# Prologue of an AdaLN and FFN kernel: agg_w in two halves around the second pair's layer 0, and W_up's load moved behind the second X

## The chip, the cores and the metric

The kernel runs on one core of one Trainium2 chip. The metric is the device time of one execution in microseconds. All data are float32. The engines are named as in the profile: PE is TensorE (PEld its weight loads), DVE is VectorE, ACT is ScalarE, POOL is GpSimd, and SP is SyncE, which only issues DMAs.

## The reference, cut to what matters

The input x has 128 samples of 64 channels and 1024 positions. Two residual layers follow each other.

```python
# layer 0: a channel mix of each sample's own, then a rank-128 product along the positions
att = softmax(mlp(cond_128))                         # 128 x 8
agg_w = einsum('bk,koi->boi', att, L0_cond_weight)   # one 64 x 64 matrix a sample
agg_b = att @ L0_cond_bias_k
y = einsum('boi,bih->boh', agg_w, x) + agg_b[:, :, None]
x = x + (y @ B) @ A.T + ffn_bias
# layer 1: a grouped convolution over 9 positions with a context a sample, then the FFN
c = conv1d(x, weight, groups=4, pad=4) + (cond_128 @ c_weight.T)[:, :, None] + fside[None, :, None]
top1 = argmax(c @ gate_w.T + expert_bias)
x = x + c @ W_up.T + lora(c, expert=top1)
```

W_up is 1024 x 1024. The kernel multiplies by its four quarters w11, w12, w21 and w22 and by sums of them (T1, T2, T3, -T4), with seven half-size products where eight would be plain.

## The kernel before, in words

Two samples make a pair of 128 rows, so there are 64 pairs, and two pairs make a group d of the FFN. Every engine's instructions stand in the order in which the program writes them: nothing is rescheduled, and each engine waits where its next instruction waits.

Layer 0 of a pair has three parts. `layer0_in` (L299) multiplies the transposed x (xt) by B in eight matmuls into pxb; ACT copies the result to xb. `layer0_mix` (L308) multiplies xb by the pair's block-diagonal agg_w into pz, and ACT or DVE makes z0 of it. `layer0_out` (L324) multiplies z0 by AT in two halves (pd), DVE adds each half to x, and SP stores it to a scratch tensor in HBM, x1d. Then SP loads it back in another layout, as X, in two DMAs (L339, L340), each of which waits for the store. The convolution `conv` works on X: pairs 0 and 1 take the plain form (L400), the later ones a form with differences made on POOL (`differences`, L355) and a shared part (`shared_in`, L366). There are three X buffers.

agg_w for all samples is made once, in `agg_all` (L273): att transposed (attT) times the weights wa in two halves of four matmuls, copied from PSUM by DVE and ACT into staging tiles and stored to HBM (`agg_out`), from where each group's matrices are loaded later (`load_cond`, L177). The first four pairs (FIRST) don't wait for this. `own_att` (L235) picks their att rows with one matmul, and `own_bd` (L248) sums their matrices in eight DVE instructions (L253 once, L255 seven times). `own_bias` (L242) makes their bias operand on ACT. `b_sums` (L225) makes the two sums of B that the biases need.

[...] Four rotate through `bank()` (pool ps); four are the FFN's accumulators, with the tags pb0 to pb3 (pool psb), which `ffn_a` (L445) first takes.

The prologue (L584 to L644) orders the loads. SP's queue carries the packed small weights, B, the first pair's xt and x, and AT; then the x1d and X transfers, smalld (the per-sample biases and contexts), their broadcasts bc, and w11. ACT's queue carries ffn_bias, xt1, wa, x1, ws, xt2 and x2. POOL's queue, after the two ffn_bias additions of pairs 1 and 2 (`add_fbias`, L550), carries w12, w22, w21, xt3, x3, gl (gate and LoRA A) and lb (LoRA B), in all 4.5 MB. The quarters' sums are made on DVE (`w_sum`, L142), and w12 lies in the buffers that the differences take later.

After the prologue a loop over d runs the FFN of group d beside layer 0 and the convolutions of the pairs to come.

Of the kernel before, what the change touches and what calls it, by code (L numbers as in the profile page):

```python
# [35 lines left out]
F32 = mybir.dt.float32  # L36
# [5 lines left out]
P = 128  # L42
# [4 lines left out]
NC = L // P  # L47
# [10 lines left out]
N = 512  # L58
GT = 64
NX = 3  # L60
NBD = 3
FIRST = 4
# [6 lines left out]
def block(ctx: ExitStack, tc: tile.TileContext, a: dict, out: bass.AP):  # L69
    nc = tc.nc  # L70
# [4 lines left out]
    psb = ctx.enter_context(tc.tile_pool(name="psb", bufs=1, space=PSUM))  # L75
# [15 lines left out]
    def bank(name):  # L91
        return ps.tile([P, 512], F32, tag="bank", name=name)

    def loaded(name, shape, src=None, tag=None, eng=nc.sync):
        t = const.tile(shape, F32, tag=tag or name, name=name)
        eng.dma_start(t, a[name] if src is None else src)
        return t
# [7 lines left out]
    def load_x(pr, eng=nc.gpsimd):  # L105
        xts[pr] = xtp.tile([P, NC, P], F32, tag="xt", name=f"xt{pr}")
        xs[pr] = xpool.tile([P, L], F32, tag="x", name=f"x{pr}")
        eng.dma_start(xts[pr], a["xt"][pr])  # L108
        eng.dma_start(xs[pr], a["x"][pr])
# [23 lines left out]
    def load_w(name, eng):  # L133
        W[name] = const.tile([P, HC, N], F32, name=f"w{name}")
        eng.dma_start(W[name], a[f"w{name}"])

    def load_w12(eng):
        for h in range(2):
            W12.append(tmp.tile([P, HC // 2, N], F32, tag=f"tmp{h}", name=f"w12_{h}"))
            eng.dma_start(W12[h], a["w12"][:, h * HC // 2 : (h + 1) * HC // 2])  # L140
# [20 lines left out]
    ones = const.tile([P, P], F32, name="ones")  # L161
# [12 lines left out]
    aggd = dram.tile([NB, CH, CH], F32, name="aggd")  # L174
    smalld = dram.tile([NB, 2, CH], F32, name="smalld")

    def load_cond(g):  # L177

        if g * GP >= FIRST:
            bds[g] = BD[g % NBD]  # L180
            for b in range(2):
                nc.sync.dma_start(
                    bds[g].rearrange("(r two) t b o -> two r t b o", two=2)[b, :, :, b, :],
                    aggd.rearrange("(t two) r o -> two r t o", two=2)[b, :, g * GP : (g + 1) * GP],
                )
        bcs[g] = bcp.tile([P, GP, 2, 2, CH], F32, tag="bc", name=f"bc{g}")
        nc.sync.dma_start(
            bcs[g].rearrange("p t b k o -> p (t b k o)"),
            smalld[2 * g * GP : 2 * (g + 1) * GP]
            .rearrange("b k o -> (b k o)")  # L190
            .unsqueeze(0)
            .partition_broadcast(P),
        )
# [29 lines left out]
    bred = const.tile([P, P], F32, name="bred")  # L223

    def b_sums():  # L225

        p = bank("pbsum")
        nc.tensor.matmul(p[:8, :P], ones[:, :8], bred, start=True, stop=True)
        nc.tensor.matmul(p[:, P : P + 1], bred, ones[:, :1], start=True, stop=True)
        nc.scalar.copy(bs8, p[:8, :P])  # L230
        nc.scalar.copy(bsum, p[:, P : P + 1])

    attx, bdx, mv = {}, {}, {}

    def own_att(pr):  # L235

        p = bank(f"pattx{pr}")
        nc.tensor.matmul(p[:, :8], sel[:, pr].rearrange("p o b -> p (o b)"), att[:, 0, :8], start=True, stop=True)
        attx[pr] = const.tile([P, 8], F32, name=f"attx{pr}")
        nc.vector.tensor_copy(attx[pr], p[:, :8])  # L240

    def own_bias(pr):  # L242

        mv[pr] = const.tile([8, 2, CH], F32, name=f"mv{pr}")
        for b in range(2):
            nc.scalar.activation(mv[pr][:, b], bk, AF.Copy, scale=attT[:8, 2 * pr + b : 2 * pr + b + 1])

    def own_bd(pr):  # L248
        bdx[pr] = const.tile([P, 2, CH], F32, name=f"bdx{pr}")
        for k in range(8):  # L250
            w = attx[pr][:, k : k + 1]
            if k == 0:
                nc.vector.tensor_scalar(bdx[pr], wk[:, k], w, None, ALU.mult)  # L253
            else:
                nc.vector.scalar_tensor_tensor(bdx[pr], wk[:, k], w, bdx[pr], ALU.mult, ALU.add)  # L255
# [5 lines left out]
    def condition_rest():  # L261

        p = bank("psmall")
        nc.tensor.matmul(p[:, :CH], attT[:8, :], bk, start=True, stop=True)
        nc.tensor.matmul(p[:, CH : 2 * CH], condT, cwT, start=True, stop=True)
        small = const.tile([NB, 2, CH], F32, name="small")
        nc.scalar.copy(small[:, 0], p[:, :CH])
        nc.vector.tensor_tensor(small[:, 1], p[:, CH : 2 * CH], fs, ALU.add)
        return small
# [3 lines left out]
    def agg_all():  # L273

        first = ytp.tile([NB, 4, 512], F32, tag="yt", name="agg0")
        second = [xpool.tile([NB, 2, 512], F32, tag="x", name=f"agg1{j}") for j in range(2)]
        for h in range(2):
            ps4 = [bank(f"pagg{h}_{j}") for j in range(4)]
            for j in range(4):
                rows = slice(32 * j, 32 * (j + 1))  # L280
                nc.tensor.matmul(ps4[j], attT[rows, :], wa[rows, h], start=True, stop=True)
            for j in range(4):
                to = second[j // 2][:, j % 2] if h else first[:, j]
                if j % 2:
                    nc.scalar.copy(to, ps4[j])
                else:
                    nc.vector.tensor_copy(to, ps4[j])
        to = aggd.rearrange("b i o -> b (i o)").rearrange("b (j h n) -> h b j n", j=4, h=2)
        aggs.extend([(to[0], first), (to[1][:, :2], second[0]), (to[1][:, 2:], second[1])])

    def agg_out():
        for to, agg in aggs:
# [12 lines left out]
        nc.scalar.copy(xb, pxb[:, :P])  # L305
        xbs[pr] = xb

    def layer0_mix(pr):  # L308
        g, t = pr // GP, pr % GP
        own = pr < FIRST  # L310
        pz = bank(f"pz{pr}")
        bd = bdx[pr] if own else bds[g][:, t]
        nc.tensor.matmul(pz[:, :P], xbs.pop(pr), bd.rearrange("p b o -> p (b o)"), start=True, stop=not own)  # L313
        z0 = z0p.tile([P, P], F32, tag="z0", name=f"z0_{pr}")
        to = z0.rearrange("k (o b) -> k b o", b=2)
        pzv = pz[:, :P].rearrange("k (b o) -> k b o", b=2)
        if own:
            nc.tensor.matmul(pz[:, :P], bs8, mv[pr].rearrange("k b o -> k (b o)"), start=False, stop=True)
            nc.scalar.copy(to, pzv)  # L319
        else:  # L320
            nc.vector.scalar_tensor_tensor(to, bcs[g][:, t, :, 0, :], bsum, pzv, ALU.mult, ALU.add)
        z0s[pr] = z0

    def layer0_out(pr):  # L324
        x, z0 = xs[pr], z0s.pop(pr)
        xt = X[pr % NX]
        d = x1d.tile([Q, P, P], F32, tag="x1d", name=f"x1d{pr}")
        dv = d.rearrange("q (c g) m -> (q c) g m", g=BG)
        h = P // 2
        for hf in range(2):  # L330
            cols = slice(hf * 512, (hf + 1) * 512)
            qs = slice(hf * Q // 2, (hf + 1) * Q // 2)
            pd = bank(f"pd{pr}_{hf}")
            nc.tensor.matmul(pd, z0, at[:, cols], start=True, stop=True)  # L334
            nc.vector.tensor_tensor(x[:, cols], pd, x[:, cols], ALU.add)  # L335
            nc.sync.dma_start(
                d[qs].rearrange("q r m -> r q m"), x[:, cols].rearrange("r (q m) -> r q m", m=P)
            )
        nc.sync.dma_start(xt[h:, :, :P], dv[:h])  # L339
        nc.sync.dma_start(xt[:h, :, 1 : P + 1], dv[h:])  # L340
# [87 lines left out]
    def conv(pr):  # L428
        for b in range(2):
            conv_in(pr, b)  # L430
            conv_out(pr, b)
# [117 lines left out]
    def add_fbias(pr, eng):  # L549
        eng.tensor_tensor(xs[pr], xs[pr], fbias, ALU.add)  # L550

    def layer0(pr):
        layer0_in(pr)
        layer0_mix(pr)
        layer0_out(pr)
# [38 lines left out]
    turn_att()  # L594
    own_bias(0)
    layer0_in(0)
    b_sums()
    own_bd(0)
    add_fbias(0, nc.vector)
    layer0_mix(0)  # L600
    small = condition_rest()
    load_x(2, nc.scalar)
    layer0_out(0)
    nc.sync.dma_start(smalld, small)
    load_cond(0)
    load_w("11", nc.sync)

    add_fbias(1, nc.gpsimd)
    add_fbias(2, nc.gpsimd)
    load_w12(nc.gpsimd)  # L610
    load_w("22", nc.gpsimd)
    load_w("21", nc.gpsimd)
    load_x(3)
    gl = loaded("gl", [P, NC, GT], eng=nc.gpsimd)
    lb = loaded("lb", [P, N], eng=nc.gpsimd)
    add_fbias(3, nc.gpsimd)
    for pr in range(1, FIRST):
        own_att(pr)
    own_bd(1)
    own_bias(1)  # L620
    layer0_in(1)
    agg_all()
    layer0_mix(1)
    layer0_out(1)
    own_bd(2)
    own_bias(2)
    own_bd(3)
    own_bias(3)
    load_cond(1)
    conv(0)  # L630
    layer0(2)
    w_sum("T1", "12", "11")
    w_sum("T2", "22", "T1")
    v = ffn_a(0)
# [132 lines left out]
```

## Time and profile before

| What | us |
|---|---|
| median of 3 runs | 1364.32 |
| lowest and highest of the 3 | 1362.79, 1369.27 |
| the profiled execution's own time | 1363.02 |
| its span | 1361.2 |
| PE busy | 1337.3 |
| DVE busy | 587.6 |
| POOL busy | 623.9 |
| ACT busy | 142.7 |

The span runs from the first to the last instruction that the profile shows; the execution's own time is 1.8 us more. A row of the timeline gives the start, the time from there to the end of the last of the instructions it merges, the engine, the line, the operation, what it writes and reads, and in brackets the idle time before it and what ended it. A row of a table by stretches gives the stretch, its length, the busy time of PE, PEld, DVE, ACT and POOL with the number of instructions, the share of the clock that TensorE was granted, the busy share of the DMA engines, and GB/s. Of the list of waits the columns are the waiting engine, tile and line, what it waited for, us in total, times, and the longest. Of the DMA queues the columns are packets, MB, and the time of the packets as a share of 16 engines over the window; q0 is POOL's queue, q1 is SP's, q10 is ACT's.

### The profile page before, as it was taken

What the parts mean: (1) busy time and instruction counts of PE and PEld (TensorE: products, weight loads), DVE (VectorE), ACT (ScalarE), POOL (GpSimd) and SP (SyncE); (2) the same over time, 40 slices, a digit from 0 to 9 for tenths busy, and PEclk for the clock granted to TensorE, in tenths of its full rate; (3) what the DMA queues carried; (4) which work ended last, traced back from release to release, by engine and by line L of the source; (5) the groups of instructions that cost most, each with busy time, mean ns of one, the idle gap of its engine ahead of it and who ended that gap; (6) DMA issues with size and microseconds to landing.
All of it is one profiled execution on the core that took longest, in us unless ns stands there. A gap on an engine that the chain in (4) does not pass through costs nothing.

```text
span 1361.2 us, 18209 instructions
## 1 busy us (share of the span) xinstructions
PE 1337.3 (98%) x7279; PEld 755.9 (56%) x7279; DVE 587.6 (43%) x980; ACT 142.7 (10%) x310; POOL 623.9 (46%) x558
## 2 busy tenths in 40 slices
PE   7799999999999999999999999999999999999997
PEld 5455455555555555555555555554555554555553
DVE  6554354443343443343443443443443443534442
ACT  2011011011011010111010110110110110110100
POOL 3364554344554344554345554445543445543322
PEclk8999999999999999999999999999999999999999
DMA  8754455444445434445444545344544344454220
GB/s 307 244 198 124 126 142 157 142 131 118 133 134 165 139 121 131 134 134 163 131 129 115 151 134 158 127 131 109 156 142 152 122 124 127 142 156 141 71 78 32
DMA packets 179414, 189.64 MB, mean 139 GB/s; under 512 B 16641, under 2 KB 148097, under 8 KB 178945
## 3 DMA queue, kind: packets, MB, share of 16 engines
q1 hardware_dynamic: 159872, 116.63, 30.9%
q0 software_dynamic: 18304, 67.64, 14.3%
q10 hardware_dynamic: 1152, 4.19, 0.9%
q8 instruction: 58, 0.95, 0.3%
q14 instruction: 28, 0.22, 0.1%
HBM read 119.16 MB, written 69.27 MB: 138 GB/s over the span
## 4 chain that ended last, share of the span: by engine, by line
PE 96%; DMA 2%; POOL 1%; DVE 1%; issue 0%; ACT 0%; DVEq 0%; ACTq 0%; POOLq 0%; SPq 0%
PE pb L436 56%; PE pxb L303 9%; PE pc L409 9%; PE pd L334 9%; PE pg L467 4%; PE pm L371 4%; PE pb L542 2%; PE pz L313 1%; DMA x1d<-x 1%; PE pgt L482 1%; PE pc L400 0%; DMA X<-x1d 0%; POOL df L364 0%; PE pzt L507 0%; POOL df L363 0%
## 5 line engine op out<-in xcount | busy, mean ns | idle before, releaser
L436 PE MATMUL pb<-wT,s 128*128 128x512 f32 x768 | 346.0, 600 | 0.0
L436 PE MATMUL pb<-w,yt 128*128 128x512 f32 x512 | 230.6, 593 | 2.2 <-DMA w<-in_w 1.5
L436 PEld LDWEIGHTS pb<-wT,s 128*128 128x128 f32 x768 | 140.8, 190 | 158.7 <-issue 158.4
L108 POOL DMA_DIRECT2D xt<-in_xt x61 | 33.6, 550 | 377.8 <-PE pxb L303 377.8
L550 POOL TENSOR_TENSOR x<-x,ffn_bias 128x1024 f32<-128x1024 f32 x63 | 148.2, 2372 | 31.0 <-DMA x<-in_x 31.0
L544 DVE TENSOR_TENSOR x<-pb,x 128x512 f32<-128x512 f32 x96 | 60.3, 684 | 230.2 <-PE pl L542 230.2
L386 DVE TENSOR_TENSOR m<-pm,bc 64x512 f32<-64x512 f32 x124 | 85.0, 686 | 167.0 <-PE pm L371 165.1
L436 PEld LDWEIGHTS pb<-w,yt 128*128 128x128 f32 x512 | 94.7, 190 | 110.4 <-issue 106.3
L335 DVE TENSOR_TENSOR x<-pd,x 128x512 f32<-128x512 f32 x128 | 88.1, 689 | 129.0 <-PE pd L334 128.9
L421 DVE TENSOR_TENSOR yt<-pc,m 128x512 f32<-128x512 f32 x124 | 124.8, 1085 | 22.6 <-PE pc L409 22.6
L334 PE MATMUL pd<-AT,z 128*128 128x512 f32 x256 | 125.6, 613 | 1.2 <-ACT z L319 1.2
L303 PE MATMUL pxb<-B,xt 128*128 128x128 f32 x1024 | 125.0, 281 | 0.2 <-DVE x L335 0.2
L409 PEld LDWEIGHTS pc<-ws,df 128*64 128x64 f32 x1984 | 107.0, 137 | 27.3 <-issue 23.5
L303 PEld LDWEIGHTS pxb<-B,xt 128*128 128x128 f32 x1024 | 118.6, 194 | 6.3 <-DVE x L544 5.1
L409 PE MATMUL pc<-ws,df 128*64 128x128 f32 x1984 | 122.0, 276 | 0.0
L436 PE MATMUL pb<-w,s 128*128 128x512 f32 x256 | 115.2, 593 | 0.7 <-DVE x L535 0.7
L436 PE MATMUL pb<-w-T,yt 128*128 128x512 f32 x256 | 115.2, 593 | 0.0
L456 POOL TENSOR_TENSOR s<-yt 128x512 f32<-128x512 f32 x32 | 40.5, 1266 | 157.1 <-DVE yt L421 157.1
L363 POOL TENSOR_TENSOR df<-X 128x512 f32<-128x512 f32 x62 | 65.4, 1055 | 97.9 <-DMA X<-x1d 92.9
L436 PEld LDWEIGHTS pb<-w,s 128*128 128x128 f32 x256 | 48.6, 190 | 62.3 <-issue 60.7
L389 ACT COPY m<-m 64x512 f32<-64x512 f32 x124 | 76.5, 617 | 58.5 <-DVE m L386 55.2
L436 PEld LDWEIGHTS pb<-w-T,yt 128*128 128x128 f32 x256 | 46.1, 190 | 55.2 <-issue 54.8
(113 smaller groups left out, 1157.6 us busy)
## 6 DMA issues: line engine op xcount, KB each, us to landing
x1d<-x SPq DMA_DIRECT2D x128, 256.0 KB, 2.3
X<-x1d SPq DMA_DIRECT2D x128, 256.0 KB, 4.0
out<-x SPq DMA_DIRECT2D x64, 512.0 KB, 2.7
xt<-in_xt POOLq DMA_DIRECT2D x61, 512.0 KB, 3.9
x<-in_x POOLq DMA_DIRECT2D x61, 512.0 KB, 4.6
bc<-smalld SPq DMA_DIRECT2D x32, 256.0 KB, 4.0
w<-in_w POOLq DMA_DIRECT2D x2, 1024.0 KB, 10.4
bd<-aggd SPq DMA_DIRECT2D x60, 32.0 KB, 4.0
```

Of the source, the lines that this page charges most:

```text
L303: nc.tensor.matmul(pxb[:, :P], xt[:, c, :], bt[:, c, :], start=(c == 0), stop=(c == NC - 1))
L334: nc.tensor.matmul(pd, z0, at[:, cols], start=True, stop=True)
L335: nc.vector.tensor_tensor(x[:, cols], pd, x[:, cols], ALU.add)
L363: nc.gpsimd.tensor_tensor(diffs[pr][:, :, 0], at_even, at_odd, ALU.subtract)
L371: nc.tensor.matmul(pm[b * H : (b + 1) * H, g * P : (g + 1) * P], blocks(pr, b, g, 1), wsum[:, g], start=True, stop=True,)
L386: nc.vector.tensor_tensor(by_group(m2[half, b]), by_group(pm[half]), context(pr, b, half), ALU.add)
L389: nc.scalar.copy(m2[other, b], m2[half, b])
L409: nc.tensor.matmul(pc[o * H : (o + 1) * H, cols], diffs[pr][:, 2 * g + b, o], ws[:, g, o], start=True, stop=True,)
L421: nc.vector.tensor_tensor(yt.rearrange("m q (o g two) -> m two g q o", two=2, g=NGC)[:, b], by_group(pcs.pop((pr, b))), context(pr, b) if ...
L436: nc.tensor.matmul(to, yt[:, c], w[:, c], start=first and c == 0, stop=c == HC - 1, skip_group_check=not first)
L544: nc.vector.tensor_tensor(x[:, cols], part, x[:, cols], ALU.add)
L550: eng.tensor_tensor(xs[pr], xs[pr], fbias, ALU.add)
```

## The change

`b_sums` becomes a generator of two parts with a PSUM bank each, and `layer0_mix(0)` runs the second part between its two matmuls. `agg_all` becomes a generator of two halves, which use the banks pb0 to pb3 in place of the rotating four. Its first half comes before `layer0_mix(1)` as before, the second now after `layer0_out(1)`. The attention rows, matrix and bias operand of pair 1 are made before `layer0_out(0)`; those of pairs 2 and 3 on either side of the first convolution, which itself moves ahead of pair 3's matrix and pair 2's layer 0. The store of smalld goes ahead of the first x1d store, and bc of the second group is loaded right after the first's. w11 goes to POOL's queue, ahead of w12. w22, w21, xt3, x3, gl and lb go from POOL's queue to SP's, behind the reload of pair 1's X. The ffn_bias addition of pair 3 on POOL follows pair 2's layer 0. The loads of pairs 4 and 5 on POOL's queue stay behind it.

```diff
     def b_sums():
+        p = bank("pbs8")
+        nc.tensor.matmul(p[:8, :P], ones[:, :8], bred, start=True, stop=True)
+        nc.scalar.copy(bs8, p[:8, :P])
+        yield
         p = bank("pbsum")
-        nc.tensor.matmul(p[:8, :P], ones[:, :8], bred, start=True, stop=True)
-        nc.tensor.matmul(p[:, P : P + 1], bred, ones[:, :1], start=True, stop=True)
-        nc.scalar.copy(bs8, p[:8, :P])
-        nc.scalar.copy(bsum, p[:, P : P + 1])
+        nc.tensor.matmul(p[:, :1], bred, ones[:, :1], start=True, stop=True)
+        nc.scalar.copy(bsum, p[:, :1])
+        yield
...
         for h in range(2):
-            ps4 = [bank(f"pagg{h}_{j}") for j in range(4)]
+            ps4 = [psb.tile([P, N], F32, tag=f"pb{j}", name=f"pagg{h}_{j}") for j in range(4)]
...
+            yield
...
-    def layer0_mix(pr):
+    def layer0_mix(pr, between=None):
...
+        if between:
+            next(between)
...
-    b_sums()
+    sums_of_b = b_sums()
+    next(sums_of_b)
     own_bd(0)
     add_fbias(0, nc.vector)
-    layer0_mix(0)
+    layer0_mix(0, sums_of_b)
+    own_att(1)
+    own_bd(1)
     small = condition_rest()
+    own_bias(1)
     load_x(2, nc.scalar)
+    nc.sync.dma_start(smalld, small)
     layer0_out(0)
-    nc.sync.dma_start(smalld, small)
     load_cond(0)
-    load_w("11", nc.sync)
+    load_cond(1)
 
     add_fbias(1, nc.gpsimd)
     add_fbias(2, nc.gpsimd)
+    load_w("11", nc.gpsimd)
     load_w12(nc.gpsimd)
-    load_w("22", nc.gpsimd)
-    load_w("21", nc.gpsimd)
-    load_x(3)
-    gl = loaded("gl", [P, NC, GT], eng=nc.gpsimd)
-    lb = loaded("lb", [P, N], eng=nc.gpsimd)
-    add_fbias(3, nc.gpsimd)
-    for pr in range(1, FIRST):
-        own_att(pr)
-    own_bd(1)
-    own_bias(1)
     layer0_in(1)
-    agg_all()
+    agg = agg_all()
+    next(agg)
     layer0_mix(1)
     layer0_out(1)
+    load_w("22", nc.sync)
+    load_w("21", nc.sync)
+    load_x(3, nc.sync)
+    gl = loaded("gl", [P, NC, GT])
+    lb = loaded("lb", [P, N])
+    next(agg)
+    own_att(2)
     own_bd(2)
     own_bias(2)
+    conv(0)
+    own_att(3)
     own_bd(3)
     own_bias(3)
-    load_cond(1)
-    conv(0)
     layer0(2)
+    add_fbias(3, nc.gpsimd)
     w_sum("T1", "12", "11")
```

More of the change, by code (lines that the diff above doesn't have):

```diff
@@ L276, in agg_all @@
         second = [xpool.tile([NB, 2, 512], F32, tag="x", name=f"agg1{j}") for j in range(2)]
+        to = aggd.rearrange("b i o -> b (i o)").rearrange("b (j h n) -> h b j n", j=4, h=2)
+        aggs.extend([(to[0], first), (to[1][:, :2], second[0]), (to[1][:, 2:], second[1])])
         for h in range(2):
-            ps4 = [bank(f"pagg{h}_{j}") for j in range(4)]
+            ps4 = [psb.tile([P, N], F32, tag=f"pb{j}", name=f"pagg{h}_{j}") for j in range(4)]
             for j in range(4):
@@ L287, in agg_all @@
                     nc.vector.tensor_copy(to, ps4[j])
-        to = aggd.rearrange("b i o -> b (i o)").rearrange("b (j h n) -> h b j n", j=4, h=2)
-        aggs.extend([(to[0], first), (to[1][:, :2], second[0]), (to[1][:, 2:], second[1])])
+            yield
     def agg_out():
```

## The prediction

> **What bounds the kernel now.** I read the page's busy times first, then TensorE's waits in the first 90 us, then a table by stretches with the granted clock, then the timeline around each wait, and last the DMA queues in short windows.
>
> ```profile
> PE 1337.3 (98%) x7279; PEld 755.9 (56%) x7279; DVE 587.6 (43%) x980; ACT 142.7 (10%) x310; POOL 623.9 (46%) x558
> ```
> TensorE is busy for 1337.3 of 1361.2 us, so 23.9 us of idle time are all that waits can give. Between 110 and 1300 us it has none (1190.00 busy of 1190). The change touches only the prologue, so the question is how much earlier the steady part starts. TensorE's waits there:
>
> ```profile
> PE pc L400 <- DMA X<-x1d: 5.1, 1, 5.1
> PE ph L197 <- DMA pk<-in_pk: 2.9, 1, 2.9
> PE pattx L238 <- DVE att L216: 1.8, 1, 1.8
> PE pagg L281 <- DVE agg L287: 1.7, 1, 1.7
> PE pb L436 <- DMA w<-in_w: 1.5, 1, 1.5
> ```
> The ph and pattx waits lie ahead of the change. The others are its targets: pair 1's convolution on its reloaded X, the second half of agg on bank copies, W_up's first quarter. The stretches show a second price, the clock (the third number from the end is the granted share):
>
> ```profile
> 24.00:31.00 7.00, 6.64 (x24) 2.86 (x22) 2.49 (x4) 2.27 (x7) 4.55 (x9) 0.57 1.03 304
> 31.00:34.00 3.00, 3.00 (x57) 2.83 (x53) 2.75 (x10) 0.00 (x0) 0.00 (x0) 1.00 1.01 404
> 51.00:56.00 5.00, 5.00 (x58) 4.64 (x56) 1.49 (x2) 0.00 (x0) 0.00 (x0) 0.71 1.04 394
> ```
> After each idle stretch TensorE runs at half clock for some us. The rows that pay, by the timeline:
>
> ```profile
> 22.45 2.55 PE L281 MATMUL pagg<-wa,attT 32*128 32x512 f32 x8 [1.68 <-DVE agg L287]
> 26.81 3.58 PE L334 MATMUL pd<-AT,z 128*128 128x512 f32 x4 [0.36 <-ACT z L319]
> 30.32 3.72 PE L400 MATMUL pc<-ws,X 128*64 128x128 f32 x64
> 50.20 5.38 PE L400 MATMUL pc<-ws,X 128*64 128x128 f32 x64 [5.08 <-DMA X<-x1d]
> ```
> The same agg matmuls took 1.55 at 19.23, pd took 1.97 at 14.49, and the same convolution 3.72 at 30.32. So the idle at 20.8 costs 1.7 and then about 3.2 of clock (1.0 agg, 0.6 two pz, 1.6 pd); the idle at 45.1 costs 5.1 and then 1.7. In all these and w11's 1.5 are 13.2 us.
>
> Why X of pair 1 is late: the chain of waits has one piece of 14.11 us, the store of x1 to x1d, issued at 31.14 behind w11 in SP's queue while POOL's queue pours 4.5 MB. Two DMA windows, 33 to 35 and 24 to 27, show how the queues share:
>
> ```profile
> q0 software_dynamic: 80, 0.64, 77.7%
> q1 hardware_dynamic: 72, 0.15, 22.3%
> ...
> q1 hardware_dynamic: 1123, 0.56, 96.5%
> q0 software_dynamic: 2, 0.01, 1.1%
> ```
> In the first, POOL's queue moves 80 packets of 8 KB and SP's 72 of 2 KB: equal in packets, not in bytes. Of 16 engines for 2 us, a share of 77.7% over 80 packets is 0.311 us a packet, and 22.3% over 72 is 0.099. In the second SP's 512 B packets run alone: 0.041 us each. From 28 to 30 us POOL's 4 KB packets cost 0.153 (98.2% of 32 us over 205).
>
> [...]
>
> ```profile
> 16.65 2.35 POOL L550 TENSOR_TENSOR x<-x,ffn_bias 128x1024 f32<-128x1024 f32 x1 [13.73 <-DMA x<-in_x]
> 17.33 1.76 DVE L253 TENSOR_SCALAR bdx<-wk,attx 128x128 f32<-128x128 f32 x1
> ```
> L253 takes 0.28 elsewhere; here it ends when POOL ends. [...]
>
> **The change, step by step.**
>
> *b_sums split, agg in banks pb0 to pb3.* The one-column matmul slips between the two pz matmuls, where TensorE waited 0.21 for ACT: nothing to 0.2 gained, taken as nothing. Agg no longer needs the four rotating banks, so its 1.7 us wait goes; its second half waits only for copies made during pair 1's layer 0. pb0 is wanted again only by w11's product, 15 us after.
>
> *own_att(1) and own_bd(1) ahead of layer0_out(0).* Now these sit in VectorE's queue before x0's two adds. VectorE is free at 14.0 (12.77 + 1.23). Copy 0.15, L253 0.28, seven L255 in 2.67, with gaps: 17.3. But POOL's add of x1 starts at 16.65 and locks out the last one or two L255 for about 2.3: 19.7. Then small 0.22 and two adds of 0.69: x0 is done at 20.6 and 21.3, not 16.3 and 17.2. The x1d stores are issued 4.2 us later. The small store that now precedes them is 128 packets, 8 an engine: 0.3, inside the same gap. Before, they took 6.3 us (16.36 issued, 22.72 its reload issued) beside ACT's x2 loads; those will be over, and the smallest landing of x1d in the trace is 2.2. So the reload of X0 is issued at about 22.9 and 23.6, against 22.72 and 23.43: covered, nearly.
>
> *w11 and w12 on POOL, the rest later on SP.* POOL issues w11 after adding to x2. x2 landed at 21.8, slowed by x1d's packets from 19 us on, which are gone; I estimate 20.3 (1 MB behind ws, which lands at 17.8, at 404 GB/s is 2.6) to 21.8. With 2.4 for the add and 2.8 from issue to first packets (issued 24.18, only 2 software packets before 27), w11's packets come at 25.5 to 27.1; I take 25.6, as the loads ahead have the engines to themselves. X0's reload is 1024 packets, 64 an engine, from 24.2 (1.3 after issue) to 26.8 alone. At 25.6 some 30 an engine are left: 8 go each behind an 8 KB packet (8 x 0.352 = 2.8), 16 each behind 4 KB of w12 (16 x 0.194 = 3.1), 6 alone 0.25. X0 lands at about 31.8. If w11 comes at 27.1, X0 lands at 27.1; if at 25.5, still about 31.8.
>
> *conv(0) moves ahead of pair 2's layer 0.* TensorE ends agg's second half and pattx at about 25.4 (pd 16.5, pxb 18.5, agg 20.1, pz 21.3, pd 23.6, agg 25.1), then waits 6.4 us for X0. After that it is cold again: 1.7 or 3.2 us by the two cases above; I take 2.5, range 1.7 to 3.4.
>
> *The sum.* Before, conv(0) starts at 30.32 and conv(1) ends at 55.5. Between them, warm and without waits for DMA, lie 3.64 + 9.65 (33.96 to 45.12 less w11's 1.51) + 3.64, and pattx3 adds 0.25: 17.2. So conv(1) ends at T + C + 17.2, with T the landing of X0 and C the clock, and the gain is 38.3 - T - C = 38.3 - 31.8 - 2.5 = 4.0 us. The later wait of 0.7 for x's add at L535 hangs on a POOL chain that starts after pair 3's add and moves along: nothing. The tail is untouched.
>
> *What comes behind X0 must keep up.* SP's queue: two bc, 16 packets an engine, 1.6; x1d of pair 1, 64 packets, 2.6: 36.0; X1's reload 4.0 (page): 40.3, wanted at 47.8. Behind it w22, w21, xt3, x3, gl, lb: 16 x (0.311 + 0.153 + 0.099) = 9.0, until 49.3; w21 about 45.3, wanted at 51; x3 with POOL's add at 51, wanted at 60. Then x1d of pair 2, 2.6, and X2 4.0: 56, or 61 when POOL's loads of pairs 4 and 5, which now wait for x3, come between (32 packets x 0.153 = 4.9). Wanted at L371: 66.4 - 4.0 = 62.4. This is the tightest cover; X2 later than that costs one for one.
>
> **Time.** The profiled execution took 1363.02 (span 1361.2), 1.3 below the median of 1364.32. Its own time less 4.0 is 1359.0; the median less 4.0 is 1360.3, which I forecast.
>
> **Rivals.**
> 1. X0 escapes W_up (w11's packets after 26.8). T = 27.1 gives 8.7, but X2 then is wanted at 57.7 and may land at 61: 5.4 to 8.7, 1355.6 to 1358.9. For it: x2's landing may not move. Against: nothing holds it once x1d's stores are late.
> 2. The wait is only moved: clock 3.4, X0 at 32.5 and some 2 us lost at X2: 0.4, 1363.9. That is a change that does not do what it says.
> 3. Slower: X2 behind W_up in the same queue. If the 3.5 MB move at the 189 GB/s of the small-packet window, they need 18.5 instead of 9.0, X2 lands at 70.4, 8.0 after it is wanted: 1364.3 - 4.0 + 8.0 = 1368.3, and 1373 if pair 3's reload behind it slips by the same 4.9 of POOL's loads. It decides from X2's landing after 66.4. Against it: these packets are 2 to 8 KB, and 404 GB/s is the rate of such stretches.
>
> **Chances.** Forecast 0.52, own range 1358.5 to 1362.5; rival 1 0.25; rival 2 0.13; rival 3 0.10. A measurement of this kernel can tell about 0.5% (6.8 us) from no change. Some 0.6 of rival 1 (0.15) and an edge of the forecast (0.05) lie beyond it below; half of rival 3 (0.05) above. Faster 0.20, same 0.75, slower 0.05. The range 1355.5 to 1364.5 leaves out rival 3 and the edges.
>
> **What would show it.** Right: conv(0) waits for DMA X<-x1d for 4 to 7 us and starts near 31.8 at half clock; L255 of pair 1 stretched by POOL; no wait of agg or w11; conv(1) without a wait; L371 within 5 us of 62. Wrong: conv(0) starting before 29 (rival 1), or a wait at L371, or any at conv(1).

## The result and the profile after

| | before | after |
|---|---|---|
| median, us | 1364.37 (14 runs, 1361.06 to 1371.61) | 1360.35 (14 runs, 1358.04 to 1361.20) |
| profiled execution, us | 1363.02 | 1360.38 |
| its span, us | 1361.2 | 1358.6 |
| conv(0) starts, us | 30.32 | 34.42 |
| conv(1) ends, us | 55.58 | 53.12 |
| first product with lb starts, us | 86.36 | 83.87 |
| from there to the end of the span, us | 1274.84 | 1274.73 |

The ratio of after to before is 0.9966, with a 95% interval from 0.9954 to 0.9978, which is 4.6 us (3.0 to 6.3); the medians of the table differ by 4.0. The two profiled executions differ by only 2.6: the one of before lies 1.35 under its median. The last row (span less start) says that everything is decided by about 85 us: the rest took 1274.5 to 1274.9 us in the profiled executions of all fourteen kernels of this study.

The page's busy times for the kernel after, to set against the first line shown of before:

```profile
PE 1336.9 (98%) x7279; PEld 757.6 (56%) x7279; DVE 586.8 (43%) x980; ACT 142.4 (10%) x310; POOL 622.1 (46%) x553
```

TensorE's busy time is the same within 0.4 us, and of its 23.9 us of idle time 21.7 are left. The list of TensorE's waits in the first 90 us:

```profile
PE pc L406 <- DMA bc<-smalld: 6.1, 1, 6.1
PE ph L197 <- DMA pk<-in_pk: 3.0, 1, 3.0
PE pattx L241 <- DVE att L216: 1.8, 1, 1.8
...
PE pb L442 <- DVE x L541: 0.7, 1, 0.7
```

The waits of agg, of w11 and of conv(1) are gone. One of 6.1 us ahead of conv(0) has come. Its label names the broadcast bc, not X; the second experiment shows that this is the wrong name. The stretches around it (the columns as before; the granted clock is third from the end):

```profile
16.00:24.00 8.00, 8.00 (x33) 4.94 (x33) 5.89 (x11) 1.32 (x5) 4.90 (x3) 1.00 0.75 244
...
28.00:34.40 6.40, 0.32 (x2) 0.24 (x3) 4.11 (x11) 2.02 (x6) 0.00 (x0) 0.79 1.02 324
34.40:40.10 5.70, 5.68 (x65) 5.53 (x65) 1.10 (x1) 0.00 (x0) 0.00 (x0) 0.64 0.68 185
...
49.40:53.10 3.70, 3.70 (x66) 3.53 (x65) 3.09 (x2) 0.59 (x1) 3.44 (x1) 1.00 0.63 198
```

TensorE no longer stops at 20 us, so both halves of agg and pair 1's pd run warm, that is at full clock (1.00 from 22 to 28 us). From 28.3 to 34.4 it does nothing while the DMA engines are full (1.02), and then runs cold, at 0.64 of its clock. The timeline's rows for the same instructions as before:

```profile
16.20 3.73 PE L340 MATMUL pd<-AT,z 128*128 128x512 f32 x4
19.72 2.79 PE L307 MATMUL pxb<-B,xt 128*128 128x128 f32 x16
22.44 1.14 PE L286 MATMUL pagg<-wa,attT 32*128 32x512 f32 x8
...
24.94 1.98 PE L340 MATMUL pd<-AT,z 128*128 128x512 f32 x4 [0.53 <-ACT z L325]
26.86 1.14 PE L286 MATMUL pagg<-wa,attT 32*128 32x512 f32 x8
...
34.42 5.70 PE L406 MATMUL pc<-ws,X 128*64 128x128 f32 x64 [6.10 <-DMA bc<-smalld]
...
49.40 3.72 PE L406 MATMUL pc<-ws,X 128*64 128x128 f32 x64
```

conv(0) now pays what conv(1) paid before, one wait and one cold convolution (5.70 against 3.72). The second half of agg has neither its wait nor the cold 2.55, and pair 1's pd takes 1.98 where it took 3.58.

The first two rows are slower than before: pair 0's pd took 1.97 there, and pair 1's pxb 2.05. The clock column says 1.00 at this time, but the trace's first record of the clock stands only at 21.46 (in before at 12.98), and up to it the matmuls take as long as cold ones: pd's last three take 1.06 us each, as pair 1's does at 27.82 in before, at a clock of 0.50; of pxb's sixteen the first seven take 0.42 us each, the last seven, from 21.56, 0.275. The change is not the reason: e1, e2 and e4 below have the same TensorE program up to here, and their pd took 1.94. This execution was slow to come up to full clock, and so TensorE finished its own work only at 28.3.

Why X0 came late, in three views: VectorE's and POOL's timeline, then SP's issues and landings in the window 23 to 26 us, then the DMA queues from 26.5 to 29.5.

```profile
15.74 4.64 DVE L258 SCALAR_TENSOR_TENSOR bdx<-wk,attx,bdx 128x128 f32<-128x128 f32 x7
...
20.43 1.28 DVE L341 TENSOR_TENSOR x<-pd,x 128x512 f32<-128x512 f32 x2
```

```profile
16.61 2.46 POOL L556 TENSOR_TENSOR x<-x,ffn_bias 128x1024 f32<-128x1024 f32 x1 [13.69 <-DMA x<-in_x]
```

```profile
w<-in_w POOLq DMA_DIRECT2D x1, 1024.0 KB, 6.1
w<-in_w POOLq DMA_DIRECT2D x2, 512.0 KB, 8.0
X<-x1d SPq DMA_DIRECT2D x2, 256.0 KB, 10.1
```

```profile
q0 software_dynamic: 167, 1.07, 91.4%
q1 hardware_dynamic: 135, 0.07, 8.7%
```

The seven sums take 4.64 us beside POOL's addition where they take 2.67 alone; x0's adds follow at 20.43, and the second half of its reload is issued at 24.08, 0.24 us behind w11. It lands at 34.17, 10.1 us later. In the last view each of the 16 engines passes 8.4 of X0's packets of 512 B while it passes 10.4 of W_up's, and these take ten times as much of the time (91.4% against 8.7%).

### The profile page after: what moved, and what is told of

The parts are those of the page before. It is cut to its first block, busy times and chain, and to the rows that moved or that the text cites. A ratio compares the mean times of both kernels' runs of the same rounds, so it can differ in the third digit from the quotient of the medians.

```text
span 1358.6 us, 18209 instructions
## 1 busy us (share of the span) xinstructions
PE 1336.9 (98%) x7279; PEld 757.6 (56%) x7279; DVE 586.8 (43%) x980; ACT 142.4 (10%) x310; POOL 622.1 (46%) x553
## 4 chain that ended last, share of the span: by engine, by line
PE 96%; DMA 1%; POOL 1%; DVE 1%; issue 0%; ACT 0%; DVEq 0%; SPq 0%; ACTq 0%; POOLq 0%
PE pb L442 56%; PE pxb L307 9%; PE pc L415 9%; PE pd L340 8%; PE pg L473 4%; PE pm L377 4%; PE pb L548 2%; PE pz L317 1%; PE pgt L488 1%; DMA bc<-smalld 1%; PE pc L406 1%; DVE bdx L258 0%; PE pzt L513 0%; POOL df L370 0%; POOL df L369 0%
## 5 line engine op out<-in xcount | busy, mean ns | idle before, releaser
L556 POOL TENSOR_TENSOR x<-x,ffn_bias 128x1024 f32<-128x1024 f32 x63 | 149.2, 2388 | 40.3 <-DMA x<-in_x 40.3
```

## The experiments

Two theories of the wait at conv(0) stood against each other. Theory A is the prediction's: it is X0's reload, slowed packet by packet by w11 and w12. Theory B takes the label at its word: it is bc. And a second question was put to all runs: if conv(0) is released, does the time come back whole, or is this wait the cover of a later one? All of them compute the full reference. The times are medians; before's in the same batches was 1363.7 to 1364.9, and each ratio is to before in the same batch. Each kernel has one profiled execution only. The columns after the ratio come from each kernel's profiled execution: when conv(0) starts, what the product with w21 and pair 2's layer-1 mix (L377, or L371 in before's numbering) wait for their load, and the start of the first product with lb.

| Kernel | us | ratio [95%] | conv(0) | w21 wait | X2 wait | lb product |
|---|---|---|---|---|---|---|
| before | 1364.4 | 1 | 30.32 | 0 | 0 | 86.36 |
| after | 1360.35 | 0.9966 [0.9954, 0.9978] | 34.42 | 0 | 0 | 83.87 |
| e1 | 1360.38 | 0.9960 [0.9945, 0.9974] | 28.48 | 3.2 | 0 | 85.53 |
| e2 | 1363.38 | 0.9979 [0.9969, 0.9988] | 31.17 | 0 | 0 | 86.77 |
| e3 | 1359.09 | 0.9950 [0.9933, 0.9967] | 28.56 | 2.7 | 0.2 | 81.76 |
| e4 | 1360.63 | 0.9955 [0.9938, 0.9972] | 28.11 | 4.1 | 2.0 | 84.51 |
| e5 | 1360.15 | 0.9970 [0.9959, 0.9981] | 32.51 | 0 | 3.5 | 85.55 |
| e6 | 1365.94 | 1.0004 [0.9991, 1.0016] | 28.07 | 0 | 0.9 | 89.43 |
| e7 | 1364.45 | 0.9995 [0.9983, 1.0008] | 29.35 | 0 | 0 | 88.91 |
| e8 | 1362.53 | 0.9982 [0.9973, 0.9991] | 29.63 | 0 | 6.1 | 84.86 |
| e9 | 1363.22 | 0.9984 [0.9975, 0.9993] | 29.34 | 0 | 0.8 | 87.81 |
| e10 | 1356.14 | 0.9942 [0.9928, 0.9957] | 32.41 | 0 | 0 | 81.55 |
| e11 | 1358.01 | 0.9952 [0.9932, 0.9971] | 31.56 | 0 | 0.2 | 80.73 |
| e12 | 1357.62 | 0.9950 [0.9932, 0.9969] | 32.03 | 0 | 0 | 81.40 |

**e1: W_up behind X0 in X0's own queue.** From after:

```diff
+    load_w("11", nc.sync)
+    load_w12(nc.sync)
     add_fbias(1, nc.gpsimd)
     add_fbias(2, nc.gpsimd)
-    load_w("11", nc.gpsimd)
-    load_w12(nc.gpsimd)
```

> The changed kernel with w11 and w12 moved from POOL's queue to SP's, behind bc, so that no W_up packet runs beside X0's reload. Theory A (X0's second half is held by W_up's packets on POOL's queue): the reload lands within about 4 us of its issue, near 28, conv(0) starts near 28 and not 34.4, and the time falls by 4 to 7 us against the changed kernel, to 1353 to 1356. Theory B (conv(0) waits for bc, as the list of waits says): bc is not held either, so conv(0) also starts early; this run does not tell A from B. Theory C (the wait for X0 is cover for something that ends as late, X1 or X2): the wait moves to L406 of pair 1 or L377 and the time stays at 1360.

X0 landed at 28.23 and conv(0) started at 28.48, 5.9 us earlier, though the second half of the reload was issued at nearly the same time (23.83 for 24.08). So W_up's packets are what held X0. But the median stayed where it was (1360.38): theory A had the start right and theory C the time. The list of waits of this run:

```profile
PE pc L406 <- DMA bc<-smalld: 3.5, 1, 3.5
PE pb L442 <- DMA w<-in_w: 3.2, 1, 3.2
```

The second line is new: the product with w21 wants it at 48.4 instead of 53.05, and it lands at 51.42. The wait and the cold product behind it (5.37 for 3.70) take back what conv(0) had won. In this execution conv(0) itself was also colder (6.63 us for 5.70), and VectorE cost 0.8 and 0.3 us more at 77 us, so that its lb product comes later than after's.

**e2: both bc loads behind X1.** From after:

```diff
-    load_cond(0)
-    load_cond(1)
...
     layer0_out(1)
+    load_cond(0)
+    load_cond(1)
     load_w("22", nc.sync)
```

> The changed kernel with both bc loads moved behind the reload of X1 in SP's queue, so that bc lands several us later. Theory A: conv(0) starts as before at 34 or up to 1 us earlier, because X0 does not wait for bc; the time stays within 2 us of 1360. Theory B (conv(0) waits for bc): conv(0) starts only when bc has landed, at 38 or later, and the time rises by about 4 us.

```profile
PE pc L406 <- DMA X<-x1d: 6.9, 1, 6.9
```

The wait stays, and without bc in the queue it bears X's name: X0 landed at 30.92, and conv(0) started 0.25 us later. In the kernel after, X0 landed at 34.17, conv(0) started 0.25 later, and bc landed only at 34.60, after the start. Theory B falls. The label comes from a shared semaphore: conv(0) also waits for ws, bc counts on the semaphore that ws used (107 in the trace of after, passed at 34.31, before bc's last count at 34.60), and the list names the transfer that counted on it last.

Theory A's numbers for e2 did not come true either. conv(0) started 3.3 us earlier than in after, where at most 1 was expected: in this execution the second half of the reload was issued 0.59 us ahead of w11, not behind it. Fifteen of the sixteen DMA engines had finished their part of it by 27.72, and the last at 30.92. And the time is 3.0 us above after's by the medians (1.8 by the ratios), where it was to stay within 2: pair 2's layer 0 now waits 3.0 for VectorE, whose yt needs bc.

**e3 and e4: the sums away from POOL's addition.** e3 puts `own_att(1)` and `own_bd(1)` back behind `layer0_out(0)`; e4 makes pair 1's bias addition on VectorE, behind x0's adds. Both from after, e3 first:

```diff
-    own_att(1)
-    own_bd(1)
...
     layer0_out(0)
+    own_att(1)
+    own_bd(1)
```

```diff
     layer0_out(0)
+    add_fbias(1, nc.vector)
...
-    add_fbias(1, nc.gpsimd)
     add_fbias(2, nc.gpsimd)
```

> The changed kernel with one part undone: pair 1's attention rows and matrix are made after layer 0 of pair 0, as before. Theory A: x0's adds end near 17.2 and not 21.7, the x1d stores land near 23 beside x2's loads, x2 lands a little later, and X0 is back at 27 to 29, just ahead of w11's packets; conv(0) starts at 27 to 30 and the time falls by 4 to 7 us against the changed kernel. If x1d's landing beside x2's loads is as late as in the changed kernel (theory D: the early matrix costs nothing, the queue order alone does), conv(0) starts at 32 or later and the time stays.

> The changed kernel with the ffn_bias addition of pair 1 moved from POOL to DVE, behind x0's adds, so that nothing locks DVE out during pair 1's L258. Theory A with the lock as its cause: the seven L258 take 2.7 and not 4.6, x0's stores are issued 2 us earlier, X0's packets are through before w11's first at 26, conv(0) starts at 26 to 29, and the time falls by 4 to 7 us. If the 2 us are not what decides: conv(0) starts above 31 and the time stays within 2 us.

In both the seven sums took 2.67 us again, X0 landed 6 us earlier than in after (28.32 and 27.86), and conv(0) followed. So X0's delay needs both, W_up's packets on POOL's queue and the 2.0 us that VectorE's sums lose beside POOL's addition (4.64 for 2.67); taking either away frees X0. How close the race is, the issues and landings of four traces show, in us:

| Kernel | x0's second store issued | reload's second half issued | w11 issued | W_up's first packet | X0 landed |
|---|---|---|---|---|---|
| after | 21.73 | 24.08 | 23.84 | 25.9 | 34.17 |
| e2 | 20.71 | 23.34 | 23.93 | 26.4 | 30.92 |
| e3 | 17.84 | 23.69 | 24.45 | 26.7 | 28.32 |
| e4 | 19.47 | 23.50 | 24.16 | 27.6 | 27.86 |

x0's second store goes out 3.9 and 2.3 us earlier in e3 and e4, but it then takes 5.8 and 4.0 us to land, not 2.3, while x2's load is still under way. So the reload is issued only 0.4 and 0.6 us earlier; w11, which follows pair 2's addition, comes 0.6 and 0.3 us later. Together that is enough: the reload is ahead of w11 by 0.76 and 0.66 us and is through as W_up's packets come. With margins this small, other executions of the same kernel may fall on the other side; no trace shows them.

Rival 1 of the prediction is thus a real state of this kernel, one order of instructions away. What it is worth is seen in the waits of e4:

```profile
PE pb L442 <- DMA w<-in_w: 4.1, 1, 4.1
PE pc L406 <- DMA bc<-smalld: 3.1, 1, 3.1
...
PE pm L377 <- DMA X<-x1d: 2.0, 1, 2.0
```

w21 and then X2 ask for the time back: 1360.63. The gain of 4 to 7 us that I expected of both did not come. e3 has the same waits in smaller numbers and ends at 1359.09, 1.3 us under after by the medians and 2.2 by the ratios; the intervals of both hold after's ratio.

**e5 and e6: the order behind it.** e5 is e3 with w21 ahead of w22; e6 is e5 with the loads of pairs 4 and 5 behind POOL's four sums for the FFN (`ffn_sums(0)`).

```diff
+    load_w("21", nc.sync)
     load_w("22", nc.sync)
-    load_w("21", nc.sync)
...
     conv(1)
-    load_x(4)
-    load_x(5)
...
         s = ffn_sums(d)
+        if d == 0:
+            load_x(4)
+            load_x(5)
```

> E3 (pair 1's matrix after layer 0 of pair 0) with w21 ahead of w22 in SP's queue. Theory A2 (once X0 comes early, the next thing late is w21, at the product L442, and behind it X2 at L377): w21 lands near 45.3 and the wait of 2.7 and its clock of 1.7 at L442 go; X2 is then wanted near 57 and lands near 60, so a wait of about 3 at L377 takes their place. The time is 0 to 2 us under E3's, 1357 to 1359. Rival (w21 was the last cover): 1354 to 1355 and no wait at L377.

> E5 with POOL's loads of pairs 4 and 5 moved behind the four sums of the FFN's group 0, so that their 4 KB packets do not run between those of X2's reload. Theory A2: X2's reload takes 4 us and not 8, lands near 57, the wait at L377 is under 1 us, and the time is 3 to 5 us under E3's, 1354 to 1356. If the loads of pairs 4 and 5 are then late themselves, a wait appears at L307 or at L541 and the gain is smaller. Rival (X2 is late because of its place behind W_up, not because of the packets between): no change against E5.

w21's wait went in both. In e5 X2's took its place: its reload was issued at 55.09 beside POOL's loads of pairs 4 and 5 and took 8.5 us. In e6, where these come later, it took 4.6 and the wait fell to 0.9. But then the delayed loads met the stores of agg on SP's queue, landed at 70.7 to 75.5, and POOL's addition of pair 4 followed only at 72.75. From e6's waits:

```profile
PE pb L442 <- DVE x L541: 9.8, 1, 9.8
```

That is the 0.7 of after's last line, grown to 9.8, and it takes the whole gain (1365.94, where I expected 1354 to 1356 or a smaller gain). The executions of e6 are not alike: three of the fourteen took 1359.1 to 1362.7, the others 1365.3 to 1367.1. e5's profiled execution also had a wait of 5.2 for bdx: this time the second of POOL's additions met the last of the seven sums (4.85 in all). Its 1360.15 lies above the 1357 to 1359 expected.

**e7 and e8: each half of the change alone**, from before. e7 takes agg's banks and its split, no queue; e8 takes the queues (w11 and w12 on POOL; w22, w21, xt3, x3, gl and lb on SP behind X1), no other order.

```diff
-            ps4 = [bank(f"pagg{h}_{j}") for j in range(4)]
+            ps4 = [psb.tile([P, N], F32, tag=f"pb{j}", name=f"pagg{h}_{j}") for j in range(4)]
...
+            yield
...
-    agg_all()
+    agg = agg_all()
+    next(agg)
     layer0_mix(1)
     layer0_out(1)
+    next(agg)
```

```diff
-    load_w("11", nc.sync)
...
+    load_w("11", nc.gpsimd)
     load_w12(nc.gpsimd)
-    load_w("22", nc.gpsimd)
-    load_w("21", nc.gpsimd)
-    load_x(3)
...
-    add_fbias(3, nc.gpsimd)
...
     layer0_out(1)
+    load_w("22", nc.sync)
+    load_w("21", nc.sync)
+    load_x(3, nc.sync)
...
     layer0(2)
+    add_fbias(3, nc.gpsimd)
```

> The kernel before with only agg's part of the change: halves in the banks pb0 to pb3, the second after layer 0 of pair 1; all queues as before. Theory A: the wait of 1.7 at agg and its clock of about 3 go, but conv(1) still waits for X1, which the queues deliver at about 50 as before, so the wait at L400 grows and the time falls by under 1.5 us: 1363 to 1365. Rival (the parts add up): 1360, 4 to 5 us faster.

> The kernel before with only the queues of the change: w11 ahead of w12 on POOL, then w22, w21, xt3, x3, gl and lb on SP behind X1's reload; agg and pair 1's matrix as before. Theory A: x0's stores go early, X0 is not held, conv(0) starts near 30 behind agg as before; X1 lands near 41, so the wait at L400 and its clock go; w21 lands near 47 and is wanted near 48. The time falls by 5 to 8 us: 1357 to 1360, at or under the whole change. If agg's halves carry the gain of the change: above 1362.

Of e7, the waits and two rows of the timeline:

```profile
PE pc L401 <- DMA X<-x1d: 6.6, 1, 6.6
...
PE pb L437 <- DMA w<-in_w: 2.9, 1, 2.9
...
PE pz L314 <- DVE bdx L255: 1.7, 1, 1.7
```

```profile
23.62 3.78 PE L335 MATMUL pd<-AT,z 128*128 128x512 f32 x4 [0.36 <-ACT z L320]
27.33 2.09 PE L283 MATMUL pagg<-wa,attT 32*128 32x512 f32 x8
```

e7 removes agg's wait of 1.7, but the next instruction waits 1.7 for bdx instead, and the cold stretch stays: pd takes 3.78 and agg's second half 2.09. So the expectation that about 3 us of clock go was wrong, though its time, 1363 to 1365, came true. The loads come no sooner: conv(1) waits 6.6 where it waited 5.1, the product with w11 2.9 where it waited 1.5, and nothing that can be told from zero is left (0.9995). e8 frees conv(0) and conv(1) of all waits, but not X2:

```profile
PE pm L371 <- DMA X<-x1d: 6.1, 1, 6.1
```

X2's second half was issued at 52.85, POOL's loads of pairs 4 and 5 from 51.84, and it landed at 63.70, 10.9 us later. My expectation of 1357 to 1360 did not foresee that. By the ratios e8 gave 2.5 us and e7 0.7 (an interval of -1.1 to 2.3), where the whole gave 4.6. In e8 what is missing is X2, in e7 X of pair 1: each half is paid only as far as the next load is in time. The early matrix of pair 1, which belongs to neither half, was not run alone.

**e9: pairs 4 and 5 between the sums**, from e5: their loads behind the second of POOL's four sums, issued at 59.26 instead of 54.70.

```diff
     conv(1)
-    load_x(4)
-    load_x(5)
...
         nc.gpsimd.tensor_tensor(s[1], s[0], a0, ALU.subtract)
+        if d == 0:
+            load_x(4)
+            load_x(5)
```

> Pair 1's bdx products after pair 0's adds, w21 ahead of w22, and POOL's loads of x4 and x5 issued after the second of its four sums of the MLP's first product, 3 to 4 us later than in the changed kernel. If only the neighbours in the queue count: X2's second half lands within 5 us of its issue, the wait of pair 2's layer-1 mix on X falls from 3.5 us to under 1, x4 and x5 land by 67, before they are wanted, and no product waits at the end of the ffn for more than 1 us: 1357 to 1359. If the queue as a whole is full up to 75 us, so that every transfer put back comes late for its own reader: the add of x4 comes late, the ffn's last step waits 3 us or more for it, and the time stays at 1360 to 1362.

X2's wait fell to 0.8, as the first case has it, and x4 and x5 landed at 65.3 and 68.9. Even so its median is 3.1 us above e5's, and above both expected ranges. Not a load, but VectorE was late:

```profile
68.23 7.40 DVE L498 TENSOR_TENSOR sc<-lg,mx 128x8 f32<-128x8 f32 x1
75.66 1.19 DVE L499 TENSOR_TENSOR sc<-sc,rank 128x8 f32<-128x8 f32 x1
```

```profile
68.97 4.63 POOL L559 TENSOR_TENSOR x<-x,ffn_bias 128x1024 f32<-128x1024 f32 x2
73.57 1.03 POOL L369 TENSOR_TENSOR df<-X 128x512 f32<-128x512 f32 x1
74.56 1.03 POOL L370 TENSOR_TENSOR df<-X 128x512 f32<-128x512 f32 x1
```

An operation on eight columns takes 7.40 us and ends when POOL's row of additions and differences ends, at 75.6. In after and in e10 the same operation stands beside the same work of POOL and takes 0.89. TensorE waited 6.1 for what comes of it (L516). By its times this is the stretch of the prediction's L253 (1.76 for 0.28) again, which ended with POOL's addition as this operation ends with POOL's row (75.63 and 75.59), in a place where neither of my two cases looked. In after the 0.89 end with the first of POOL's two additions (71.52 and 71.50). What holds the operation no view shows, and why it came through there and not here stays open.

**e10: no meeting of POOL's addition and the sums**, from e9: pair 1's bias addition on VectorE, pair 2's on POOL behind the issues of w11 and w12.

```diff
     own_bd(1)
+    add_fbias(1, nc.vector)
...
-    add_fbias(1, nc.gpsimd)
-    add_fbias(2, nc.gpsimd)
     load_w("11", nc.gpsimd)
     load_w12(nc.gpsimd)
+    add_fbias(2, nc.gpsimd)
```

> The same as the run before, with pair 1's ffn_bias add on VectorE after its bdx products, and pair 2's on POOL behind the issues of w11 and w12, so that POOL's add meets none of the bdx products. If that lock is what the 2 to 5 us of the waits for bdx were: the seven products take 2.7 us in all, the first product of pair 1's layer 0 waits under 1.5 us for bdx, and the time is 1355 to 1358. If the queue is full: 1359 to 1362, with a wait for X2, x4 or w22 of 3 us or more in place of it.

This is the fastest kernel of the study, 1356.14, but not for the reason I had written. With no addition ahead of them, POOL issued w11 and w12 at 2.85 us, before anything of the kernel's own inputs was in. They landed by 20.3. The price and what is left of waits:

```profile
PE pd L340 <- DMA AT<-in_AT: 3.1, 1, 3.1
PE ph L197 <- DMA pk<-in_pk: 2.9, 1, 2.9
PE pc L406 <- DMA X<-x1d: 2.3, 1, 2.3
...
PE pb L442 <- DVE x L544: 0.7, 1, 0.7
...
PE pz L317 <- DVE bdx L258: 0.3, 1, 0.3
```

AT is 3.1 late. X0 is 2.3 late without a packet of W_up beside it. w21 and X2 are in time, and the lb product starts at 81.55. This trace is of one of e10's slower executions (1358.09), so it does not show where the last 2 us of its median come from.

**e11 and e12: the same loads on ScalarE's queue**, issued at 8.9 us directly behind ws: e11 from after, e12 from e10.

```diff
     ws = loaded("ws", [P, NGC, 2, P], eng=nc.scalar)
+    load_w("11", nc.scalar)
+    load_w12(nc.scalar)
...
-    load_w("11", nc.gpsimd)
-    load_w12(nc.gpsimd)
```

> The changed kernel with one thing moved: w11 and w12 (8 packets per engine of 2.8 and 2 times 1.5 us, some 8.6 us of transfers) leave POOL and are issued on ScalarE's queue directly behind ws, near 9 us, when no other load is due; nothing is left between X0's reload and X1's but the bc loads and pair 1's stores. If the queue's order and not its total is what decides: X0's second half lands 4 to 5 us after its issue, conv(0) starts near 29 to 31, w21 and X2 land 5 to 9 us earlier than in the runs that only released conv(0), no product waits for W_up, and the time is 1354 to 1357. If the queue is full from its start: the loads of pair 1's and pair 2's inputs or x0's stores move back by the same 8 us, layer 0 of pair 1 or conv(0) takes the wait, and the time is 1359 to 1362.

> The run with pair 1's bias add on VectorE, which by the way let POOL issue w11 and w12 at 2.9 us, ahead of AT (1356.1, with a wait of 3.1 us for AT), now with these loads on ScalarE's queue behind ws, as in the run beside it. If the order decides: no wait for AT, pair 1's layer 0 without a wait for bdx, conv(0) near 29, and 1352 to 1355. If the queue's total decides: 1355 to 1358, with the 3 us taken by another load.

From e11:

```profile
PE pc L406 <- DMA X<-x1d: 5.4, 1, 5.4
...
PE pb L442 <- DVE x L541: 0.3, 1, 0.3
PE pm L377 <- DMA X<-x1d: 0.2, 1, 0.2
```

AT is in time again. But W_up and the second input pair now fill the engines until 25.6, and x0's store, issued at 20.36, lands at 26.19 where it took 2.2 us in after. X0 lands at 31.43. e11's median, 1358.01, lies between its two cases: the loads behind X0 are all in time, as the first has it; the wait for X0 comes back by way of its store, as the second has it. e12, at 1357.62, is its second case: AT is in time, and X0 is 5.5 late instead. e11 moves two lines of after and takes 2.3 us off its median (1.9 by the ratios), but the intervals of e11 and e12 both hold after's ratio. No version was found without an idle TensorE somewhere between 14 and 36 us.

## Why the prediction was right, and which of its terms were not

**The time** held: 1360.35 against 1360.3 forecast. The mechanism was that of the likeliest case: no wait of agg, of w11 or of conv(1); the sums of pair 1 stretched by POOL; conv(0) held by X0 for 6.1 us, under bc's name, and then cold; the mix of pair 2 at 63.95, within 5 us of 62. One mark was missed: conv(0) starts at 34.42, not near 31.8. And one was met by luck: the wait was to be 6.4 us, but TensorE was ready for conv(0) at 28.3 and not at 25.4, because this execution came up to full clock so late. It was about as late as X0, so the wait between the two kept its size.

**T was too small by 2.6 us.** What the sums lost beside POOL's addition (4.64 less 2.67 is 2.0, for 2.3), x0's adds (done at 21.1 and 21.7, for 20.6 and 21.3) and the issue (24.08 for 23.6) were right within 0.5. The prices of the packets held: beside w11 each of X0's packets cost an engine 0.356 us (48 us over 135, in the view shown), for 0.352; beside w12 a pair cost 0.205 (73.0% of 48 us over 213 packets and 31.5% over 381, from 30 to 33 us), for 0.194. Two things were mis-sized. When W_up's first packet came, at 25.9, 454 of X0's 1024 packets had passed, so that some 36 an engine were left, for 30. With these counts and prices I estimate the last packet at 32.5 (25.9 + 2.8 + 3.3 + 0.5); it ended at 33.2. And the landing counted only at 34.17, 1.0 us after the last packet. The working ends with the last packet and has no term for this. It is not peculiar to this kernel: in e1, e3 to e6 and e9 to e12 X0's landing follows its last packet by 0.8 to 1.2 us. The 0.7 us between 32.5 and 33.2 stay open.

**C and the rest were too large by a little.** The cold convolution cost 1.98 (5.70 less 3.72), for 2.5, and conv(1) ends at 53.12, which leaves 16.7 for the 17.2 of the working. Together: 53.12 where the sum had 51.5. In the pair of profiled executions the gain is therefore 2.5 us at the lb product and 2.6 in all, not 4.0. That the medians differ by 4.0 all the same rests on before's profiled execution, which lies under its median. The ratio's interval starts at 3.0, above the 2.6 of the two traces. Which part of that difference is the scatter of single executions is not settled; all that the traces can account for is 2.6. That the forecast was met within 0.1 us is therefore luck; that it was met within its range is not.

**One step moved nothing.** conv(0) stood ahead of pair 2's layer 0 in before already (30.32 against 33.96); what moved behind it is pair 3's attention rows and matrix. The sum is not touched by this.

**What comes behind X0** kept up, but not for all of the reasons given. Landed for forecast: X1 42.3 for 40.3, w21 47.1 for 45.3, X2 56.7 for 56 to 61, each about 2 late with X0 itself. X2 was at the early end because POOL's loads of pairs 4 and 5 came only at 53.5, behind POOL's addition of pair 3, which itself took 3.94 where pair 2's took 2.34. I had called X2 the tightest cover. w21 was tighter: it had 6 us in hand (47.1, wanted at 53.05), and e1, e3 and e4, which start conv(0) 5.9 to 6.3 earlier, all ran into it, since it then lands later too (47.9 to 51.4).

**Rival 1** was priced at 1355.6 to 1358.9. Its mechanism exists (e1, e3, e4), but the time is 1359.1 to 1360.6: the working saw X2 behind it and not w21 ahead of X2. **Rival 3**'s mechanism, X2 too late, exists as well (e5, e8), by POOL's loads and not by the rate of W_up's packets; it is worth 3.5 to 6.1 us of wait and does not appear in after. **Rival 2**, only moved, is what e7 is: 1364.45.

**Where the expected gain goes.** Of the 13.2 us of waits and clock that the change removes, conv(0) takes 6.1 and 2.0 back. The slow start of this execution takes some 2.5 more, by my estimate: the cold stretches that went (4.9) less the new one (2.0) should have cut TensorE's busy time by 2.9, and it fell by 0.4. Had TensorE been warm, it would have waited for X0 that much longer. What is left is the 2.6 of the two traces. Releasing conv(0), in three ways (e1, e3, e4), gave at most 1.3 us by the medians, because the next load becomes late. What moved the medians further was to use the DMA engines earlier (e10, e11, e12, by 4.2, 2.3 and 2.7 us under after's): they are full from 28 to 34 us and again from 40 to 49 (1.02 and 1.01 in after), and W_up can be loaded before. Of these three, e10 alone has an interval that leaves out after's ratio.

## What to carry to other kernels

When a prologue is a chain of loads, a wait is also the cover of the loads behind it. Before pricing its removal, list for each later load when it lands and when it is then wanted, and take the smallest difference; here it was 6 us for w21, and so a release of 6 us gave at most 1.3. Adding an early load is not free either: look for who stores or reloads through the same engines at that time (x0's store went from 2.2 to 5.8 us).

## What the runs showed of the hardware

- VectorE's operation beside POOL's work was stretched, once, over more than one of POOL's instructions: in e9 a 128x8 operation took 7.40 us and ended with the last of four of POOL's in a row (75.63 and 75.59). The same operation took 0.89 in after and e10, and 0.34 at the shortest (32 times in before, 0.34 to 1.31).
- The clock around conv(0) in the kernel after can be dated by finer stretches:

```profile
30.00:34.40 4.40, 0.00 (x0) 0.02 (x1) 2.19 (x7) 0.07 (x1) 0.00 (x0) 0.69 1.04 318
34.40:37.00 2.60, 2.58 (x24) 2.60 (x26) 0.00 (x0) 0.00 (x0) 0.00 (x0) 0.50 0.77 228
37.00:40.00 3.00, 3.00 (x43) 2.88 (x40) 1.10 (x1) 0.00 (x0) 0.00 (x0) 0.74 0.61 149
```

  A mean of 0.69 over 4.4 us is 1.7 us at full and 2.7 at half, the 0.50 of the second row: the clock fell at 31.7, 3.4 us after the last matmul ended at 28.3. 0.74 over 3.0 us is a rise at about 38.5, 4.1 us after conv(0) began. Between the two lie 6.8 us. In before, found in the same way, it fell at 23.2, rose at 30.0, fell at 50.5 and rose at 53.9: 6.8, 20.5 and 3.4 us apart. Of before's two falls the first came 2.4 us after TensorE had stopped (20.8; it worked again from 22.45), the second 5.4 us after (45.1), and the idle of 1.5 us from 39.94 was followed by none: the clock stays at 1.00 up to 50.5. The prediction's "after each idle stretch" is too wide, then, and no one length of idle that brings the clock down is shown. The price of a wait varies too: conv(0) behind a wait of 2 to 7 us took 5.14 us (e4), 5.38 (e10), 5.70 (after), 6.14 (e2) and 6.63 (e1), for 3.72 warm.
- The half reloads of X in the first 70 us of after took 3.7 to 5.5 us where no packet of POOL's ran beside them, and 8.5 to 10.9 beside POOL's loads of 4 and 8 KB packets (after, e5, e8).
- X0's second half counted as landed with the last of its sixteen engines: in after their sixteen counts came from 33.44 to 34.17, and TensorE passed its wait for it at 34.20; in e2 fifteen had finished by 27.72, and the last came 3.2 us later.
- From POOL's issue of W_up to its first packet 2.1 to 3.4 us passed (2.1 in after, 2.8 in before, 3.4 in e4).
